# A three-stage convolution block on one core: one x tile per block of v, another order of loads, and products that nobody reads

## The chip, the cores and the metric

The kernel runs on one core of a Trainium2 chip. The metric is the time on the device in microseconds (us), the median of several runs. The core has four engines with instruction queues of their own: TensorE (PE: matrix products, and PEld: loads of their weights), VectorE (DVE), ScalarE (ACT) and GpSimd (POOL), and SyncE (SP), which here only starts DMA transfers. ACT and POOL start transfers too. [...]

## The reference: two residual blocks on one image

Input x has 384 channels of 192 x 192 float32. Group normalisation (32 groups of 12 channels) stands ahead of both blocks.

```python
def L0(x):                       # x = x + L0(gn(x))
    qkv = einsum('bchw,oc->bohw', x, w_qkv) + b_qkv        # 1x1, 384 -> 1152
    qkv = maxpool 2x2 (192 -> 96)
    qkv = depthwise 3x3 (qkv, w_dw) + b_dw
    q, k, v = split(qkv); q, k normalised over the pixels
    attn = q k^T * temperature   # 8 heads, 48 x 48 channels
    out = sum over 4 sizes of topk_softmax(attn, kk) @ v * a
    out = gelu(out); repeat each pixel 2 x 2
    return einsum('bchw,oc->bohw', out, w_proj) + b_proj
def L1(x):                       # x = x + L1(gn(x))
    w_sym = mean of the four rotations of weight
    return depthwise 7x7 (x, w_sym), padding 3
```

## The kernel before

Channels lie on the 128 partitions, in KT = 3 tiles. The program has stages, one after another on TensorE, with seams where they meet.

**Statistics and q, k.** x is read once for the mean and deviation of the first normalisation. Then, for 24 blocks of 8 image rows, TensorE forms q and k (`pq`, L639), VectorE takes the 2x2 maximum (L647) and the depthwise taps (`qk`, L682), ScalarE the squares for the norms (`junk`, L691), and TensorE transposes q and k (`tr`, L700) and adds their products to the attention's matrix (`grams`, L709). `depthwise(b - 1, ...)` runs a block behind. In the pass after the last block (b == NB) six groups of products of v are begun from a tile `xv_begun`, two after every second depthwise: `convolve(0, t0, n % KT, ...)`. A group is one call of `convolve`: 2 x 3 products of 384 columns (`pv`, L537) and one maximum (`rows`, L543).

**The attention**, a generator `attention`, is advanced by a few steps after each group of products of v: the norms' sum `rn` (L771), its root (POOL, L772), its reciprocal, `along_free` (L216), which lays three columns of rn along the free axis by three products with diagonal matrices (`dg_rk` L223, `af_rk` L224), the scaled matrix (L788), transfers that gather it by heads, ranks and softmaxes (`gt`, L813 and after), and its transpose `aT` (L857).

**v and the residual.** The image's 192 rows are cut in 6 tiles of 32 rows; a block is 2 rows of each of the 6 (NBC = 16 blocks). For each block three tiles `xv` of two row groups each are loaded (`load_v`, L876, three transfers of 384 KB each), and three tiles `xr` of one channel tile and all six row groups for the residual (`load_r`, L998, 1152 KB each). Both come from one pool of 6 places (tag "xv"), which the allocator hands out as they come free. Every x value of a block is thus read twice. Per iteration of the loop over i: convolutions of block i, depthwise taps `vb` (L903) of blocks i-1 and i-2, attention and projection of block j = i-2 (`po`, L959; `pr`, L983; `y`, L991), and its residual: `sx` = x + y (L1017, four additions for each channel tile, three `sx` buffers in turn), squares for the second statistics (ScalarE, L1037), and the writing of sx to DRAM (`sd`, L1058, and its halo rows `sh`), issued by POOL. After the loop come the last taps, all together, and the residuals of three blocks: NBC-2, NBC-1 and NBC (a wrap-around of the order).

**Second statistics.** Sums over groups by small products: `gs_mid` (L1237's input) and `gs`, both at L185; then `norm_of` (L211 to L215, with a power on POOL), and `along` (L1262), three times for channel tile 0: mean (`mb`), deviation (`sb`), its inverse (`rb`), each a diagonal on VectorE, a product `al` (L1266) and a copy. `masked` (L1271), `middle` (adds the deviation to the middle tap of w, L1253) and three rows of offsets (`offs`, L1294 and L1299, written by ScalarE's queue to h and to `wh`) follow.

**The 7x7 convolution**, 48 steps of 8 channels. A step has 4 groups q; a group forms 2 x 3 products of 288 columns into `pc`: w with main (L1389), w with main one column on (L1394), h with aux (L1400), in this order for each channel. `main` and `aux` come from sd and sh (`load_main`, `load_aux`), `w` and `h` from prepared weights; POOL corrects their borders (`borders`, L1310 to L1337), ScalarE copies rows of main into aux (`rest`, L1349) and columns of w into h (`columns`, L1187). Loads of steps 0 and 1 are issued by SP, later ones by ScalarE's queue (`queue`, L1161):

```python
        ws = {n: load_w(n) for n in range(2)}
        ws = {n: (ws[n], load_h(n)) for n in range(2)}
        auxes = {n: load_aux(n) for n in range(2)}
        mains = {n: (load_main(n), auxes[n]) for n in range(2)}
```

VectorE and ScalarE take the sums out of PSUM (`apart`, L1411, L1413), POOL interleaves them, SP writes them out.

**The order of work.** `keep` (or `pin`) makes an instruction stay in its place in the program; `tc.issue_after(x)` puts what is in it behind x; where neither stands, the order within an engine is chosen at build time by a planner from its own estimates of when operands are ready. A tile in a pool of n places waits for the release of the tile n earlier in its place.

## Time and profile before

| | us |
|---|---|
| median of 3 runs | 2817.28 (2816.37 to 2819.05) |
| profiled execution | 2823.79 |
| its span | 2822.1 |
| TensorE busy | 2640.9 (94%) |
| VectorE busy | 2320.9 (82%) |
| ScalarE, POOL busy | 870.5, 761.4 |

The profile shows one execution; its durations add up to the span of 2822.1, not to the median. PE and DVE are engines, "idle before" is the engine's idle time ahead of a group of instructions, and what follows the arrow is the instruction that ended it. PEclk is the TensorE clock granted, as a share of full speed: at half the clock a product takes twice as long. A line number is that of the kernel before. Products are recorded in two halves, so that x12 in a timeline of TensorE is six products of `convolve`.

The stages in the profiled execution: statistics up to about 120 us, q and k to about 1390, v and the residuals to 2217, the second statistics to 2230, the 7x7 steps to 2806, and the last results out until 2822.1.

### The profile page before, as it was taken

The page shows a single profiled execution, that of the slowest core. Times are in us where ns is not written, and L with a number is a line of the kernel's source. Part 1 is how long each engine was busy: PE and PEld are TensorE (multiplying, and loading weights), DVE is VectorE, ACT ScalarE, POOL GpSimd, SP SyncE. Part 2 cuts the span into 40 slices and gives each one's busy share as a digit, 9 for nine tenths or more (in the row PEclk, how much of TensorE's full clock was granted, in tenths as well). Part 3 has the DMA queues.
Part 4 walks back from the last instruction along what each step waited for, and adds up shares of the span by engine and source line. Part 5 has one row for each costly group of instructions (what it writes and reads, how often), then busy time and mean ns, then how long its engine had stood idle before and what let it go on. Part 6 is the DMA issues. An engine that isn't in the chain of part 4 may idle for free.

```text
span 2822.1 us, 25467 instructions
## 1 busy us (share of the span) xinstructions
PE 2640.9 (94%) x8671; PEld 1582.7 (56%) x8671; DVE 2320.9 (82%) x3382; ACT 870.5 (31%) x1637; POOL 761.4 (27%) x884
## 2 busy tenths in 40 slices
PE   0399999999999999999999999999998699999997
PEld 0144444444445444444556666666666477777775
DVE  7989887887878878778698888888889678777886
ACT  0141111111111111111202232322324567777775
POOL 1034444100000000000102230100101467888886
PEclk9999999999999999999999999999999799999999
DMA  9976766301001011010235998575666899999997
GB/s 377 400 244 219 258 200 219 126 34 67 34 34 67 34 51 50 34 67 1 80 124 189 332 376 293 199 251 179 235 207 224 301 304 362 372 373 370 373 373 248
DMA packets 236353, 584.52 MB, mean 207 GB/s; under 512 B 16656, under 2 KB 168064, under 8 KB 219456
## 3 DMA queue, kind: packets, MB, share of 16 engines
q1 hardware_dynamic: 175296, 286.77, 29.1%
q0 software_dynamic: 37376, 148.85, 15.2%
q10 hardware_dynamic: 23552, 147.27, 13.9%
q8 instruction: 69, 1.13, 0.2%
q14 instruction: 60, 0.49, 0.0%
HBM read 374.47 MB, written 208.21 MB: 206 GB/s over the span
## 4 chain that ended last, share of the span: by engine, by line
PE 89%; DVE 6%; DMA 3%; POOL 1%; issue 1%; ACT 0%; ACTq 0%; POOLq 0%; SPq 0%; DVEq 0%
PE pq L639 38%; PE pv L537 18%; PE pc L1400 6%; PE pc L1389 6%; PE pc L1394 6%; PE pr L983 4%; PE po L959 3%; DMA xs<-in_x_dram 2%; PE grams L709 2%; PE tr L700 2%; PE pq_begun L423 1%; DVE st L318 1%; DVE vb L903 1%; DVE sx L1017 1%; DMA bp<-in_bproj_dram 1%
## 5 line engine op out<-in xcount | busy, mean ns | idle before, releaser
L639 PE MATMUL pq<-xq,wq 128*128 128x512 f32 x2268 | 990.7, 592 | 0.0
L639 PEld LDWEIGHTS pq<-xq,wq 128*128 128x128 f32 x2268 | 423.2, 190 | 492.0 <-issue 446.8
L682 DVE SCALAR_TENSOR_TENSOR qk<-ring,wd,qk 128x384 f32<-128x384 f32 x1152 | 676.1, 615 | 20.9 <-ACT ring L669 7.1
L537 PE MATMUL pv<-xv,wq 128*128 128x384 f32 x1656 | 540.7, 487 | 3.2 <-DVE rows L543 3.0
L647 DVE TENSOR_REDUCE ring<-pq 128x128 f32<-128x512 f32 x428 | 294.7, 689 | 190.5 <-PE pq L639 188.8
L537 PEld LDWEIGHTS pv<-xv,wq 128*128 128x128 f32 x1656 | 314.8, 190 | 218.3 <-DVE rows L543 5.0
L1413 DVE TENSOR_SCALAR apart<-pc,rb 32x576 f32<-32x576 f32 x384 | 312.0, 813 | 125.7 <-PE pc L1400 111.4
L1411 ACT ACTIVATE apart<-pc,rb 32x576 f32<-32x576 f32 x384 | 281.1, 732 | 144.5 <-PE pc L1400 139.7
L903 DVE SCALAR_TENSOR_TENSOR vb<-rows,wd,vb 128x576 f32<-128x576 f32 x384 | 313.3, 818 | 11.3
L1400 PE MATMUL pc<-aux,h 128*128 128x288 f32 x768 | 250.9, 408 | 2.7 <-POOL aux L1322 2.7
L1389 PE MATMUL pc<-main,w 128*128 128x288 f32 x768 | 251.4, 409 | 0.3 <-issue 0.3
L1394 PE MATMUL pc<-main,w 128*128 128x288 f32 x768 | 251.3, 409 | 0.0
L1017 DVE TENSOR_TENSOR sx<-xr,y 128x576 f32<-128x576 f32 x192 | 217.4, 1173 | 33.8 <-ACT y L991 21.4
L691 ACT ACTIVATE junk<-qk 128x384 f32<-128x384 f32 x144 | 75.3, 523 | 548.8 <-DVE qk L682 548.8
L801 POOL MEMSET lower<- 128x2304 f32 x1 | 2.0, 2017 | 881.1 <-ACT rows L508 881.1
L1359 POOL COPY res<-apart 128x1152 f32<-128x1152 f32 x96 | 210.0, 2222 | 87.2 <-DMA out_dram<-res 61.0
L1058 POOL DMA_DIRECT2D sd<-sx x96 | 72.2, 756 | 491.8 <-DVE sx L1017 474.2
L543 DVE TENSOR_REDUCE rows<-pv 128x192 f32<-128x768 f32 x144 | 137.8, 957 | 54.2 <-PE pv L537 54.1
L1400 PEld LDWEIGHTS pc<-aux,h 128*128 128x128 f32 x768 | 146.3, 191 | 45.5 <-POOL aux L1322 3.5
L1394 PEld LDWEIGHTS pc<-main,w 128*128 128x128 f32 x768 | 146.7, 191 | 41.9
L1389 PEld LDWEIGHTS pc<-main,w 128*128 128x128 f32 x768 | 146.4, 191 | 41.9 <-issue 0.6
L1037 ACT ACTIVATE wq<-sx,negmid 128x1152 f32<-128x1152 f32 x96 | 120.6, 1256 | 96.6 <-DVE sx L1017 92.5
(216 smaller groups left out, 2384.5 us busy)
## 6 DMA issues: line engine op xcount, KB each, us to landing
sd<-sx POOLq DMA_DIRECT2D x96, 600.0 KB, 10.1
xr<-in_x_dram SPq DMA_DIRECT2D x48, 1152.0 KB, 14.1
out_dram<-res SPq DMA_DIRECT2D x192, 288.0 KB, 8.4
main<-sd ACTq DMA_DIRECT2D x46, 1200.0 KB, 9.8
xv<-in_x_dram SPq DMA_DIRECT2D x138, 384.0 KB, 5.4
xq<-in_x_dram SPq DMA_DIRECT2D x21, 2304.0 KB, 8.2
w<-wt ACTq DMA_DIRECT2D x46, 1024.0 KB, 6.6
xs<-in_x_dram SPq DMA_DIRECT2D x24, 1536.0 KB, 15.1
```

Of the source, the lines that this page charges most:

```text
L537: nc.tensor.matmul(ps[:, u, 0 : RB * HW], wq[:, kt, o : o + P], xb[:, kt, u, :], start=(kt == 0), stop=(kt == KT - 1),)
L639: nc.tensor.matmul(ps, wq[:, kt, ct * P : (ct + 1) * P], rows[:, kt, :, g * 64 : (g + 1) * 64], start=(kt == 0), stop=(kt == KT - 1), skip ...
L647: nc.vector.tensor_reduce(t[:, r0 : r0 + PR, 1 + g * 32 : 1 + (g + 1) * 32], ps.rearrange("p (h a w b) -> p h w a b", h=PR, a=2, b=2), AX. ...
L682: nc.vector.scalar_tensor_tensor(dst, src, w, dst, ALU.mult, ALU.add)
L903: pin(nc.vector.scalar_tensor_tensor(dst, src, w, dst, ALU.mult, ALU.add))
L1017: nc.vector.tensor_tensor(bass.AP(flat.tensor, flat.offset + at(e) + a * RUN, [flat.ap[0], [JP, NT], [1, NJ], [at(f) - at(e), 2]],), xq[:, ...
L1359: keep(nc.gpsimd.tensor_copy(res[:, k], apart[:, :, k].rearrange("p e n -> p n e")))
L1389: nc.tensor.matmul(acc, w[:, i, 0:P], main[:, i, :, 0:NJ], start=True, stop=False)
L1394: nc.tensor.matmul(acc, w[:, i, P : 2 * P], main[:, i, :, 1 : 1 + NJ], start=False, stop=False,)
L1400: nc.tensor.matmul(acc, h[:, i], aux[:, i, :, 0:NJ], start=False, stop=True,)
L1411: keep(nc.scalar.mul(dst, src, scale))
L1413: keep(nc.vector.tensor_scalar_mul(dst, src, scale))
```

## The change

- **The seam from q, k to v.** The six begun groups are called at ct = 2 (two), ct = 4 (two), ct = 5 and ct = 6 (one each), inside `issue_after(multiplied)`: `multiplied` is the last gram of block 22 up to ct = 5, and that of block 23 at ct = 6, so five groups come behind the one and the sixth behind the other. `rn` moves to the pool of constants, and the diagonal `dg` has three buffers instead of two.
- **x of v.** One tile `xv` with a fixed place for each pair of row groups takes the place of the xv tiles out of the common pool; `xr` has a pool of 3. The residual of the last block in the loop's order reads its x from this tile, and its three xr loads are gone. In `xv_begun` and `xv` the row groups are the outer index and the channel tiles the inner one.
- **The last taps.** The taps dy = 0 of block NBC come after the second residual of block NBC-2.
- **The first loads of the 7x7 stage.** SP now issues w0, h0, h1, aux0, main0, w1, aux1, main1; before it was w0, w1, h0, h1, aux0, aux1, main0, main1. The three transfers of offsets go from ScalarE's queue to SP's.
- **Products nobody reads.** `busy` forms products of the resident projection weights into a PSUM tile of its own: 16 after gs_mid, 2 before the al of the mean, 2 before that of the deviation, 3 before that of its inverse.
- **Step 0.** Groups 0 and 1 form all their products of w and main (eight) before those of h and aux.

Places and counts that follow from these in the build, per engine: VectorE has as many instructions as before, TensorE 23 products more; POOL clears two of the three h tiles ahead of its last six sd transfers; VectorE forms the deviation's diagonal and the first offsets ahead of the copy of mb, and the other offsets and rb ahead of the middle taps of w.

The diff, with one line of context:

```diff
@@ -219,7 +219,7 @@
         for t in range(KT):
-            dg = const.tile([P, P], F32, name=f"dg_{name}_{t}", tag="dg", bufs=2)
+            dg = const.tile([P, P], F32, name=f"dg_{name}_{t}", tag="dg", bufs=KT)
             nc.vector.tensor_scalar_mul(dg, ident, src[:, t : t + 1])
@@ -535,7 +535,7 @@
                     nc.tensor.matmul(
-                        ps[:, u, 0 : RB * HW], wq[:, kt, o : o + P], xb[:, kt, u, :],
+                        ps[:, u, 0 : RB * HW], wq[:, kt, o : o + P], xb[:, u, kt, :],
                         start=(kt == 0), stop=(kt == KT - 1),
@@ -729,9 +729,9 @@
                 pv = psx.enter_context(tc.tile_pool(name="pv", bufs=2, space=PSUM))
-                xb = xpool.tile([P, KT, 2 * UT, RB * HW], F32, name="xv_begun", tag="xb")
+                xb = xpool.tile([P, 2 * UT, KT, RB * HW], F32, name="xv_begun", tag="xb")
                 for kt in range(KT):
-                    nc.sync.dma_start(xb[:, kt], image_rows(kt, order[0], 0, 2 * UT))
+                    nc.sync.dma_start(xb[:, :, kt], image_rows(kt, order[0], 0, 2 * UT))
             qk = []
@@ -748,12 +748,13 @@
                     depthwise(b - 1, ct - 1, dst)
-                    if b == NB and ct % 2 == 0:
-                        for n in range(ct - 2, ct):
-                            t0 = n // KT * UT
-                            convolve(0, t0, n % KT, xb[:, :, t0 : t0 + UT], lambda ins: ins)
                     if ct == 2 * KT:
                         multiplied = products(b - 1, qk)
+                    if b == NB:
+                        with tc.issue_after(multiplied):
+                            for n in ((), (), (0, 1), (), (2, 3), (4,), (5,))[ct]:
+                                t0 = n // KT * UT
+                                convolve(0, t0, n % KT, xb[:, t0 : t0 + UT], lambda ins: ins)
             if b == 2:
@@ -767,7 +768,7 @@
-        rn = ap.tile([P, 2 * KT], F32, name="rn")
+        rn = const.tile([P, 2 * KT], F32, name="rn")
         nc.vector.tensor_reduce(rn, ssq, AX.X, ALU.add)
@@ -866,7 +867,9 @@
     vp = dx.enter_context(tc.tile_pool(name="vp", bufs=6))
-    xp2 = dx.enter_context(tc.tile_pool(name="xp2", bufs=6))
+    xp2 = dx.enter_context(tc.tile_pool(name="xp2", bufs=3))
+    xvp = dx.enter_context(tc.tile_pool(name="xvp", bufs=1))
+    xvs = xvp.tile([P, NT, KT, RB * HW], F32, name="xv")
     H = PBC // 2
@@ -874,10 +877,9 @@
     def load_v(i, t0):
-        b = order[i]
-        xb = xp2.tile([P, KT, UT, RB * HW], F32, name=f"xv{b}_{t0}", tag="xv")
+        xb = xvs[:, t0 : t0 + UT]
         for kt in range(KT):
-            nc.sync.dma_start(xb[:, kt], image_rows(kt, b, t0, UT))
+            nc.sync.dma_start(xb[:, :, kt], image_rows(kt, order[i], t0, UT))
         return xb
@@ -996,7 +998,10 @@
     def load_r(i, ot):
-        xr = xp2.tile([P, NT, RB * HW], F32, name=f"xr{order[i % NBC]}_{ot}", tag="xv")
+        if i == NBC - 1:
+            return xvs[:, :, ot]
+        xr = xp2.tile([P, NT, RB * HW], F32, name=f"xr{order[i % NBC]}_{ot}", tag="xr")
         nc.sync.dma_start(xr, image_rows(ot, order[i % NBC], 0, NT))
@@ -1105,7 +1110,8 @@
-    for j, dys in ((NBC - 2, (2,)), (NBC - 1, (0, 1)), (NBC, (0,))):
+    for j, dys in ((NBC - 2, (2,)), (NBC - 1, (0, 1))):
         for ct in range(KT):
@@ -1119,6 +1125,9 @@
             next(after[ot])
+            if (j, ot) == (NBC - 2, 1):
+                for ct in range(KT):
+                    depthwise_v(NBC, ct, (0,), keep)
         before = after
@@ -1160,9 +1169,8 @@
-            if n < 2:
-                return nc.sync.dma_start
-            return lambda dst, src: keep(nc.scalar.dma_start(dst, src))
+            engine = nc.sync if n < 2 else nc.scalar
+            return lambda dst, src: keep(engine.dma_start(dst, src))
@@ -1197,10 +1205,13 @@
-        ws = {n: load_w(n) for n in range(2)}
-        ws = {n: (ws[n], load_h(n)) for n in range(2)}
-        auxes = {n: load_aux(n) for n in range(2)}
-        mains = {n: (load_main(n), auxes[n]) for n in range(2)}
+        ws, mains = {0: load_w(0)}, {}
+        hs = [load_h(n) for n in range(2)]
+        for n in range(2):
+            ws[n] = ws[n] if n == 0 else load_w(n), hs[n]
+            aux = load_aux(n)
+            mains[n] = load_main(n), aux
@@ -1231,10 +1242,17 @@
         rstd1 = const.tile([P, KT], F32, name="rstd1")
+        def busy(ps, n):
+            for _ in range(n):
+                keep(nc.tensor.matmul(ps[:, 0:H], wp[:, 0, 0:P], wp[:, 1, 0:H], start=True, stop=True))
         with tc.tile_pool(name="gps1", bufs=1, space=PSUM) as gps:
             nc.vector.tensor_scalar_mul(gmid, ps[:, :, 0], 1.0 / GC)
+            busy(gps.tile([P, 512], F32, name="busy"), 16)
             ps = over_groups(gps, about(mv1, gmid, "1"), 2, "gs1")
@@ -1277,10 +1295,14 @@
+        idle = pc.tile([P, 2, 512], F32, name="idle", tag="pc")
+        busy(idle[:, 0], 2)
         along(mb, mean1, 0)()
+        busy(idle[:, 0], 2)
         masked(0)
         along(sb, std1, 0)()
+        busy(idle[:, 0], 3)
         middle(0)
@@ -1293,11 +1315,11 @@
         for n in ws:
-            nc.scalar.dma_start(ws[n][1][ONE : ONE + 1], offs[span(n), 0, :])
+            nc.sync.dma_start(ws[n][1][ONE : ONE + 1], offs[span(n), 0, :])
         along(rb, rstd1, 0)()
             nc.vector.tensor_scalar_mul(offs[:, kt, :], ones, off1[:, kt : kt + 1])
-        nc.scalar.dma_start(wh[ONE - TOP].rearrange("(t p) n -> p t n", p=P), offs)
+        nc.sync.dma_start(wh[ONE - TOP].rearrange("(t p) n -> p t n", p=P), offs)
@@ -1380,28 +1402,32 @@
             apart = outp.tile([P, CP, 2, NT * NJ], F32, name=f"apart{n}", tag="apart", bufs=3)
-            for q in range(CP):
-                ps = pc.tile([P, 2, 512], F32, name=f"pc{n}_{q}", tag="pc")
+            ahead = {}
+            def sums(q, steps):
+                if q not in ahead:
+                    ahead[q] = pc.tile([P, 2, 512], F32, name=f"pc{n}_{q}", tag="pc")
                 for k in range(2):
                     i = 2 * q + k
-                    acc = ps[:, k, 0 : NT * NJ]
-                    keep(
-                        nc.tensor.matmul(
-                            acc, w[:, i, 0:P], main[:, i, :, 0:NJ], start=True, stop=False
+                    for j in steps:
+                        lhs, rhs = (
+                            (w[:, i, j * P : (j + 1) * P], main[:, i, :, j : j + NJ]) if j < 2
+                            else (h[:, i], aux[:, i, :, 0:NJ])
                         )
-                    )
-                    keep(
-                        nc.tensor.matmul(
-                            acc, w[:, i, P : 2 * P], main[:, i, :, 1 : 1 + NJ],
-                            start=False, stop=False,
+                        keep(
+                            nc.tensor.matmul(
+                                ahead[q][:, k, 0 : NT * NJ], lhs, rhs,
+                                start=(j == 0), stop=(j == 2), skip_group_check=True,
+                            )
                         )
-                    )
-                    keep(
-                        nc.tensor.matmul(
-                            acc, h[:, i], aux[:, i, :, 0:NJ],
-                            start=False, stop=True,
-                        )
-                    )
+                return ahead[q]
+            if n == 0:
+                for q in range(2):
+                    sums(q, range(2))
+            for q in range(CP):
+                ps = sums(q, range(2 if q in ahead else 0, 3))
                 c = n * CB + 2 * q
                     src = ps[g * TR : (g + 1) * TR, :, 0 : NT * NJ]
```

## The prediction

> **What bounds the kernel now.** I read the page's busy shares and slices first, to find out which engine sets the time and where it doesn't, then its groups.
>
> ```profile
> PE 2640.9 (94%) x8671; PEld 1582.7 (56%) x8671; DVE 2320.9 (82%) x3382; ACT 870.5 (31%) x1637; POOL 761.4 (27%) x884
> PE   0399999999999999999999999999998699999997
> PEclk9999999999999999999999999999999799999999
> L537 PE MATMUL pv<-xv,wq 128*128 128x384 f32 x1656 | 540.7, 487 | 3.2 <-DVE rows L543 3.0
> L1017 DVE TENSOR_TENSOR sx<-xr,y 128x576 f32<-128x576 f32 x192 | 217.4, 1173 | 33.8 <-ACT y L991 21.4
> ```
>
> TensorE is full nearly everywhere: from 1500 to 2140 us its busy time is 640.00 of 640.00, from 2294 to 2806 it is 512.00 of 512.00. An edit there pays only if it shortens TensorE's own work. Time can be won at the seams: the change from q,k to v (1390 to 1450), and slices 30 and 31 (2117 to 2258, the 8 and the lone 7 of PEclk), with the end of v, the second statistics and the first 7x7 step.
>
> Seam one, TensorE's timeline (start, length, line, count, idle before and its releaser):
>
> ```profile
> 1368.99 19.51 PE L537 MATMUL pv<-xv_begun,wq 128*128 128x384 f32 x60
> 1388.34 1.67 PE L700 MATMUL tr<-ident,qk 128*128 128x128 f32 x12
> ...
> 1401.28 1.19 PE L224 MATMUL af_rk<-dg_rk,ones 128*128 128x128 f32 x4 [3.89 <-DVE dg_rk L223]
> ...
> 1403.97 39.79 PE L537 MATMUL pv<-xv,wq 128*128 128x384 f32 x120
> 1446.80 3.49 PE L537 MATMUL pv<-xv,wq 128*128 128x384 f32 x10 [3.05 <-DVE rows L543]
> ```
>
> Two stalls, 3.89 and 3.05. What holds dg_rk is seen on ScalarE and VectorE:
>
> ```profile
> 1388.54 0.51 ACT L508 ACTIVATE rows<-ones,negb 128x16 f32<-128x16 f32 x2 [7.49 <-PE pv L537]
> ```
>
> ```profile
> 1394.35 0.30 DVE L771 TENSOR_REDUCE rn<-ssq 128x6 f32<-128x144 f32 x1 [4.85 <-ACT rows L508]
> ```
>
> The norms' sum rn waits for border fills, though its last square was done at 1381.05; the attention's first big operation (gt, L813) starts only at 1410.13.
>
> Seam two, VectorE's residual additions sx:
>
> ```profile
> 2169.06 13.53 DVE L1017 TENSOR_TENSOR sx<-xr,y 128x576 f32<-128x576 f32 x12
> 2184.48 4.61 DVE L1017 TENSOR_TENSOR sx<-xr,y 128x576 f32<-128x576 f32 x4 [1.89 <-DMA sd<-sx]
> ...
> 2200.65 4.58 DVE L1017 TENSOR_TENSOR sx<-xr,y 128x576 f32<-128x576 f32 x4 [2.20 <-DMA sd<-sx]
> 2206.73 4.55 DVE L1017 TENSOR_TENSOR sx<-xr,y 128x576 f32<-128x576 f32 x4 [1.50 <-ACT wq L1037]
> 2212.44 1.15 DVE L1017 TENSOR_TENSOR sx<-xr,y 128x576 f32<-128x576 f32 x1 [1.17 <-DMA sd<-sx]
> ```
>
> The last ends at 2217.0. Three sx buffers go round, and each waits until its write to sd has landed; the DMA share is 1.01 (2200 to 2216). Behind it hangs everything, on TensorE's timeline:
>
> ```profile
> 2201.93 2.00 PE L185 MATMUL gs_mid<-mid,gsel 128*128 128x1 f32 x14 [2.33 <-ACT y L991]
> 2219.23 3.15 PE L185 MATMUL gs<-about,gsel 128*128 128x2 f32 x14 [15.30 <-DVE about L205]
> ...
> 2234.74 1.30 PE L1400 MATMUL pc<-aux,h 128*128 128x288 f32 x2 [2.70 <-POOL aux L1322]
> ...
> 2240.63 0.72 PE L1400 MATMUL pc<-aux,h 128*128 128x288 f32 x2
> ```
>
> After 15.30 us idle the granted clock is 0.50 from 2205 to 2240: a 7x7 product takes 0.96 us until 2240.8, then 0.485. From 2293.64 on nothing waits, so a microsecond won before that is won at the end.
>
> **The change, part by part.**
>
> *One xv tile, three xr buffers.* Products, loads and bytes per block stay; only the row order inside the tile turns, and a product still reads 384 elements in a row (487 ns). Each place is reloaded once per block (50.35 us) and waits only for the last product that read the same place a block before; from the order on SP's queue each load has 38 us or more of lead against a landing of 5.4: 0. The last block's residual reads x from the tile: three loads of 1152 KB fall away, 3 x 1152 KB at 376 GB/s = 9.4 us of DMA time near 2102 to 2165, hidden there, but lightening the stretch whose landings hold sx.
>
> *The seam q,k to v.* Of six begun groups (3.87 us each) five now come before the last block's transposes and the sixth after its grams; rn no longer waits for the fills and the depthwise has two instead of three reduces of 0.96 between its taps. rn can be summed at 1381.1; with POOL's power (1.36) and two small operations it is there at 1384, long before TensorE asks. Five groups end as before at about 1388.3; transposes, tps and grams take 5.3 (5.7, less one transpose trio done earlier), af_rk 1.0, groups six and 13_4_0 7.74: 13_4_1 starts at 1402 instead of 1403.97, **-2.0**. The fourth group's place is taken by waiting (the first group no longer fills gaps between block 22's transposes, 3.9 us), which is why the 3.89 isn't won whole. The attention chain starts some 10 us earlier (rkb and scaled right after af_rk, then the same 4 us of att DMAs), on a VectorE that idles 17 us between 1381 and 1410; the stall at 1446.80 comes from that chain's lateness and goes: **-3.0**. Together -5.0; bounds -2 (the stall stays) and -6.5.
>
> *The end of v.* Nine taps of block NBC (7.4 us; vb L903 at 0.82) move behind two residuals. VectorE's work is the same: 33 taps from 2142.0 (27.2) and 36 additions of 1.155 (41.6) end at 2210.8 if nothing waits; now it is 2217.0. sx starts at 2161.6; buffers come round by 4.5 us of additions, with the nine taps in the second turn, so the fourth and fifth residuals find landings of 10 us done; from the sixth on 1 to 4 us of waiting remain at 9.6 to 12.8 us a landing. I take 2.5: the end is 2213.3, **-3.7** (-1 to -6).
>
> *Loads of the first steps.* SP's order is now w0, h0, h1, aux0, main0, then w1, aux1, main1. main0 waits for the sd writes, and 2.8 MB now stand behind that wait: 7.5 us at 376 GB/s. With main0 issued by 2213 to 2216 they land by 2227; POOL asks for main1 at 2231.53 and VectorE for w1 at 2242.28, so 0; 5 us later they would bind. The three offset DMAs go from ScalarE's queue to SP, whose next work is the outputs: ScalarE's copies for step 0 (they stood 13.02 us idle behind offs L1299) start 0.9 us earlier. POOL clears h0 and h1 before the last sd issues, in idle of 5 us, so that the power no longer stands behind six memsets: -0.4.
>
> *Products nobody reads.* 16 after gs_mid, then 2, 2 and 3 ahead of the three al products. Shape 128x288 as pc: 0.485 warm, 0.96 cold. 16 take 7.8 to 15.4 us from about 2200; gs can't start before 2215.5, so they fit unless all are cold. What they buy hangs on the clock. The row: after 2234.74 the clock came back in 6.1 us of unbroken products. [...] By the row the 16 take 6.1 + 9.6 x 0.485 = 10.8[...]: done by 2211, so TensorE idles 4 us before gs[...]: the clock may have fallen again. The trace agrees (the 3.57 us idle at 2144.66 is followed by 0.52). I take gs as cold (3.15, no gain) and the seven small ones, with al, as dense work from the norms to step 0, 7 us, which by the row wakes it: step 0 warm. Cold they delay rb by 1 us: **+0.5**. If the clock holds, gs is 1.1 shorter.
>
> *Step 0.* Eight products of w and main come first; aux is wanted 3.9 us (warm) after the first, and comes 4.1 after: the 2.70 becomes 0.2. VectorE now makes three small operations and the first offsets ahead of mb (about 1 us), rb ahead of w: w comes within 0.8 us of before, taken as 0. Steps 0 to 2 take 42.1 us from 2229.78, at 0.485 they are 34.9: 7.2 lost, 2.7 by the wait and 4.5 by the clock. **-6.0** warm (7.2 less 0.2 and a last half-cold stretch of 1), -3.5 cold.
>
> Sum: -5.0 - 3.7 - 0.4 + 0.5 - 6.0 = -14.6. The profiled execution takes 2823.79 (span 2822.1 and 1.7 around it), 6.5 above the median of the runs, 2817.28; so 2809.2 in its terms and **2802.7 us** as a median.
>
> **Rivals.** *Half of it*: the landings still pace sx (DMA share 1.01 speaks for it) and step 0 is cold: -5 - 1 - 3.5 + 1 = -8.5, 2808.8. *Nothing*: 1446's stall stays, the dummies run cold to 2215.4 and hold gs, w1 and main1 arrive late by 3 to 5 us: -2 - 1 + 2 - 3.5 + 4 = -0.5, 2816.8. *More*: landings free sx wholly and the cold stretch at 2276 (2.9 us, after step 2's al) goes as well: -20, 2797. *Slower*: SP's queue is in order, and a v load stands behind xr loads that wait for a residual a block back. If a load landed later than its 38 us of lead, each of 13 iterations would stall. From (14.6 + 5.6)/13 = 1.6 us apiece the kernel is slower; at the 5.4 us of a whole load it is +70 - 15, 2872. Against it: VectorE, which releases xr, idles 74 of 640 us in the loop.
>
> **How the numbers follow.** Forecast 0.60 (own range 2798 to 2807), half 0.20, more 0.06, nothing 0.08, slower 0.06. The measurement can tell 0.2%, 5.6 us: faster below 2811.6, slower above 2822.9. Forecast, more, and most of half are faster: 0.85; same 0.09, slower 0.06. The range, 2795 to 2812, leaves out nothing and slower and a little of more.
>
> **What would show it.** rn near 1381; no stall over 1 us near 1440, aT near 1480 (before 1485.61). sx ends 2 to 5 us nearer the last tap of v. No 15 us idle before gs, but one of 2 to 5; the first pc at 0.485, no aux wait over 1. From step 3 the same 11.64 a step. It is wrong if TensorE in the v loop is no longer full, if pc starts at 0.96, or if the wait moves to w1 or main1.

## The result and the profile after

The changed kernel takes 2804.3 us (median of 5 runs, 2802.2 to 2807.42) against 2818.65 for the kernel before beside it: ratio 0.9948, 95% interval 0.9936 to 0.996, or 14.35 us. The forecast was 14.6 us and 2802.7. The profiled execution has a span of 2802.6; that of before had 2822.1, 19.5 more. The 5 us beyond the medians' difference come from the choice of execution: the profiled one of before (2823.79) lies 5.1 above this median, that of the changed kernel (2804.3) is its median.

The page of the changed kernel, its busy shares and slices:

```profile
PE 2647.1 (94%) x8717; PEld 1586.9 (57%) x8717; DVE 2352.2 (84%) x3382; ACT 870.7 (31%) x1637; POOL 745.6 (27%) x884
...
PE   0399999999999999999999999999999899999997
...
PEclk9999999999999999999999999999999999999999
```

TensorE is busy 6.2 us longer, for 23 products more and others warmer or colder, and the 7 of PEclk is gone. TensorE's timeline at the seam from q, k to v (start, length, line, count, idle before it and what ended it):

```profile
1364.45 19.51 PE L537 MATMUL pv<-xv_begun,wq 128*128 128x384 f32 x60
1383.80 1.04 PE L700 MATMUL tr<-ident,qk 128*128 128x128 f32 x8
...
1388.49 0.94 PE L224 MATMUL af_rk<-dg_rk,ones 128*128 128x128 f32 x6
...
1403.21 47.02 PE L537 MATMUL pv<-xv,wq 128*128 128x384 f32 x144 [1.36 <-DVE rows L543]
```

The 3.89 at af_rk is gone, and so is the 3.05 at 1446.80; a new wait for rows, of 1.36, stands at 1403.21. VectorE there:

```profile
1377.13 0.29 DVE L772 TENSOR_REDUCE rn<-ssq 128x6 f32<-128x144 f32 x1
...
1395.03 4.79 DVE L814 TENSOR_TENSOR gt<-att 128x2304 f32<-128x2304 f32 x1
```

rn no longer waits for the fills, and gt starts at 1395.03 instead of 1410.13; since the last q,k product is 5.4 us earlier in this execution, 9.7 of the 15.1 are the seam's. (gt takes 4.79 here and 2.56 before; POOL works on `lower`, L803, beside it, from 1394.93 to 1397.40.) VectorE's residual additions after the loop:

```profile
2162.18 7.39 DVE L905 SCALAR_TENSOR_TENSOR vb<-rows,wd,vb 128x576 f32<-128x576 f32 x9
...
2186.76 4.62 DVE L1022 TENSOR_TENSOR sx<-xv,y 128x576 f32<-128x576 f32 x4 [3.81 <-DMA sd<-sx]
2192.70 10.06 DVE L1022 TENSOR_TENSOR sx<-xr,y 128x576 f32<-128x576 f32 x9 [1.33 <-DMA sd<-sx]
```

The nine taps stand between the residuals, and two waits for landings remain, 5.1 us. The second statistics and step 0 on TensorE:

```profile
2195.41 9.69 PE L1249 MATMUL busy<-wp 128*128 128x288 f32 x32
2208.36 2.53 PE L185 MATMUL gs<-about,gsel 128*128 128x2 f32 x14 [3.26 <-DVE about L205]
2211.15 2.29 PE L1249 MATMUL idle<-wp 128*128 128x288 f32 x4 [0.26 <-DVE norm L211]
...
2215.96 1.62 PE L1249 MATMUL idle<-wp 128*128 128x288 f32 x6
...
2219.26 4.12 PE L1419 MATMUL pc<-main,w 128*128 128x288 f32 x16 [1.46 <-POOL aux L1352]
2223.38 2.18 PE L1419 MATMUL pc<-aux,h 128*128 128x288 f32 x8
```

The 15.30 us of idle are 3.26, the 16 products (32 halves) take 9.69, the eight of step 0 take 4.12, 0.51 apiece, and those of aux follow without a wait.

Laid side by side by stages, with a second trace of each kernel (the runs e1 and e5 below), in us:

| stage | before | before again | changed | changed again |
|---|---|---|---|---|
| start to first q,k product | 122.5 | 121.5 | 121.5 | 122.0 |
| to the end of the last one (first tr of block 22) | 1237.8 | 1238.1 | 1233.3 | 1231.4 |
| to aT | 125.4 | 125.0 | 122.3 | 120.7 |
| to the first tap after the loop | 656.4 | 656.4 | 656.4 | 662.6 |
| to the end of the last sx | 75.0 | 75.1 | 72.6 | 72.7 |
| to the first pc | 12.8 | 12.8 | 13.1 | 12.2 |
| to the end of step 2 | 42.1 | 42.1 | 35.4 | 35.4 |
| to the end | 550.2 | 551.0 | 547.9 | 548.7 |

### The profile page after: what moved, and what is told of

The parts are those of the page before. It is cut to its first block, busy times and chain, and to the rows that moved or that the text cites. A ratio compares the mean times of both kernels' runs of the same rounds, so it can differ in the third digit from the quotient of the medians.

```text
span 2802.6 us, 25628 instructions
## 1 busy us (share of the span) xinstructions
PE 2647.1 (94%) x8717; PEld 1586.9 (57%) x8717; DVE 2352.2 (84%) x3382; ACT 870.7 (31%) x1637; POOL 745.6 (27%) x884
## 3 DMA queue, kind: packets, MB, share of 16 engines
q8 instruction: 69, 1.13, 0.2%
## 4 chain that ended last, share of the span: by engine, by line
PE 89%; DVE 6%; DMA 3%; issue 1%; POOL 0%; ACT 0%; ACTq 0%; POOLq 0%; SPq 0%; DVEq 0%
PE pq L639 37%; PE pv L537 20%; PE pc L1419 20%; PE pr L985 4%; PE po L961 3%; DMA xs<-in_x_dram 2%; PE grams L709 2%; PE tr L700 2%; PE pq_begun L423 1%; DVE qk L682 1%; DVE st L318 1%; DVE sx L1022 1%; DVE vb L905 1%; DMA bp<-in_bproj_dram 1%; DMA sd<-sx 0%
## 5 line engine op out<-in xcount | busy, mean ns | idle before, releaser
L1419 PE MATMUL pc<-main,w 128*128 128x288 f32 x1536 | 434.8, 405 | 1.8 <-POOL aux L1352 1.5
L905 DVE SCALAR_TENSOR_TENSOR vb<-rows,wd,vb 128x576 f32<-128x576 f32 x384 | 313.2, 817 | 11.2
L1381 POOL COPY res<-apart 128x1152 f32<-128x1152 f32 x96 | 222.6, 2344 | 21.6 <-ACT apart L1437 18.9
L1022 DVE TENSOR_TENSOR sx<-xr,y 128x576 f32<-128x576 f32 x180 | 203.6, 1173 | 27.3 <-ACT y L993 21.3
L1271 DVE SCALAR_TENSOR_TENSOR w<-eye,sb,w 128x512 f32<-128x512 f32 x96 | 168.0, 1789 | 1.5
L1419 PEld LDWEIGHTS pc<-aux,h 128*128 128x128 f32 x768 | 144.9, 189 | 42.1 <-issue 0.9
L985 PE MATMUL pr<-gl,wp 128*128 128x288 f32 x576 | 142.6, 406 | 0.0
```

Source lines behind the costliest of these rows:

```text
L905: pin(nc.vector.scalar_tensor_tensor(dst, src, w, dst, ALU.mult, ALU.add))
L985: nc.tensor.matmul(ps[:, 0:H], wp[:, ct, ot * P : (ot + 1) * P], gl[:, ct, h * H : (h + 1) * H], start=(ct == 0), stop=(ct == KT - 1),)
L1022: nc.vector.tensor_tensor(bass.AP(flat.tensor, flat.offset + at(e) + a * RUN, [flat.ap[0], [JP, NT], [1, NJ], [at(f) - at(e), 2]],), xq[:, ...
L1271: nc.vector.scalar_tensor_tensor(mid, eye.unsqueeze(1).to_broadcast([P, 4, P]), sb[:, c : c + 1], mid, ALU.mult, ALU.add,)
L1381: keep(nc.gpsimd.tensor_copy(res[:, k], apart[:, :, k].rearrange("p e n -> p n e")))
L1419: nc.tensor.matmul(ahead[q][:, k, 0 : NT * NJ], lhs, rhs, start=(j == 0), stop=(j == 2), skip_group_check=True,)
```

## The experiments

The ratios are to the kernel before, timed beside each. Its median was 2818.65, 2818.82, 2831.78, 2828.02 and 2817.81 us in the five groups of runs, so that times of different groups aren't compared; the stages of the traces are the finer gauge.

| run | ratio (95%) |
|---|---|
| changed | 0.9948 (0.9936 to 0.996) |
| e1 before again | 0.9997 (0.9987 to 1.0008) |
| e2 no products | 0.9964 (0.9952 to 0.9976) |
| e3 groups back | 0.9939 (0.9923 to 0.9954) |
| e4 taps back | 0.9973 (0.9963 to 0.9984) |
| e5 changed again | 0.9932 (0.9909 to 0.9955) |
| e6 rn back | 0.9981 (0.9968 to 0.9994) |
| e7 loads back | 0.9932 (0.9906 to 0.9958) |
| e8 step 0 back | 0.9953 (0.9941 to 0.9965) |
| e9 xv back | 0.9966 (0.9953 to 0.9978) |
| e10 xr by POOL | 0.9955 (0.9942 to 0.9967) |
| e11 groups back, xr by POOL | 0.9942 (0.9928 to 0.9955) |
| e12 no sixteen | 0.9956 (0.994 to 0.9972) |

### Both kernels a second time (e1, e5)

> The kernel before, unchanged, for a second trace. The two profiled executions differ by 19.5 us in span, the medians by 14.35; 4.4 us of the difference lie between the first q,k product and the last one, which no part of the change touches (two stalls there in the trace of before, 2.08 at L639 and 1.74 at L700). Theory A, they are the chance of one execution: here the time from the first pq_begun to the last pq is 1233 to 1236 us in place of 1237.8, and the span near 2817. Theory B, the new build's order or addresses removed them: the two stalls come back and the span is again near 2822.

> The changed kernel, unchanged, beside the next three, and for a second trace. By the six traces so far the time from the first pq_begun to the last pq is of two kinds in kernels whose code up to there is the same (1231 to 1233 us in two, 1237 to 1238 in four). Theory A, it is the chance of an execution: the median is again 2804 (2802 to 2806), whichever kind the trace shows. Stages after it, as in the first trace: last pq to first tap vb after the loop 778 to 780, from there to the last sx 72.6, sx to the first pc 13, steps 0 to 2 35.4. Theory B, a build's addresses decide it: the trace shows 1233 again.

Before again has 1238.1 us from first to last q,k product and both stalls (2.08 and 1.96), so e1's theory A, as put, fell. Its theory B forecast them, but that the new build had removed them by its order fell with e2, e4, e8, e11 and e12: in their traces, with the code of the changed kernel up to there, this stage takes 1237 to 1238 too, and in seven others with that code 1231 to 1234.

What the stalls are can be read from the traces. VectorE and POOL of before at the second one, then VectorE of changed again at the same instruction:

```profile
338.24 2.20 DVE L680 TENSOR_SCALAR qk<-ring,wd,bdb 128x384 f32<-128x384 f32 x1
```

```profile
338.05 2.18 POOL L566 MEMSET g<- 128x2496 f32 x1 [8.71 <-DMA wt<-g]
```

```profile
333.00 0.48 DVE L680 TENSOR_SCALAR qk<-ring,wd,bdb 128x384 f32<-128x384 f32 x1
```

By itself this operation takes 0.46 to 0.48 us in all fourteen traces. In before it starts at 338.24, inside POOL's memset (338.05 to 340.23, which prepares weights of the 7x7 stage), and ends at 340.44, 0.21 us behind it, and TensorE waits for what follows. In the first traces of the two kernels all twelve operations of this line that start inside such a memset end behind it. The first stall stands in eleven of the fourteen traces, and the operation takes 1.87 to 2.55 us there; the second in seven, with 2.20 to 2.48; where a stall is missing, it takes 0.82 at most in the same place. Who goes first is a matter of nanoseconds: at the first stall the operation starts 0.148 us ahead of the memset in before and takes 2.54; in the changed kernel it starts 0.160 ahead and takes 0.48, and the memset takes 2.43 instead of 2.18. Throughout the fourteen traces a start up to 0.157 ahead was held, and one from 0.160 on was not.

With neither stall the stage takes 1231.4 to 1233.3 (the changed kernel twice, e3), with the first alone 1233.7 to 1233.9 (e6, e7, e9, e10), with both 1237.2 to 1238.1. Up to 1300 us the instructions of all four engines stand in the same order in all fourteen traces, so no edit acts there; what differs is when two operations meet. Each of the two kernels showed its own kind twice, so whether the executions of one kernel change between the kinds isn't shown. That stays open, and with it some 5 us of the difference between the traces.

Changed again has a median of 2813.48, outside e5's 2802 to 2806, but before took 2831.78 beside it; the ratio is 0.9932, where it was 0.9948. And it brought what I had set at 0: the loop takes 662.6 instead of 656.4. TensorE's timeline of e5:

```profile
1666.68 0.88 PE L537 MATMUL pv<-xv,wq 128*128 128x384 f32 x2 [1.88 <-DMA xv<-in_x_dram]
1668.50 25.74 PE L537 MATMUL pv<-xv,wq 128*128 128x384 f32 x70 [0.93 <-DMA xv<-in_x_dram]
```

SP's queue in the same execution:

```profile
1613.94 22.39 SPq L1005 DMA_DIRECT2D xr<-in_x_dram  x3
1636.42 34.10 SPq L882 DMA_DIRECT2D xv<-in_x_dram  x9
```

The first of these xv loads, from the view of its line between 1636 and 1637:

```profile
DMA to landing us min/median/max: 30.1/30.1/30.1
```

The place was free when the product group before it ended, at 1626 (1614.29 and a group of 11.6). The load stood behind three xr loads waiting for sx until 1636.4, and landed at 1666.5, when TensorE had been waiting since 1664.8. So the lead of 38.8 us was there, as predicted; 10.4 of it went to SP's queue and 30.1 to a landing put at 5.4. After the 1.88 us of idle the clock was down, as the sums over three stretches show (length; busy time of PE, PEld, DVE, ACT, POOL with counts; the granted clock; DMA share and GB/s):

```profile
1664.13:1667.54 3.41, 1.53 (x5) 0.49 (x3) 3.36 (x4) 2.79 (x5) 2.96 (x4) 1.00 1.06 404
1667.54:1674.37 6.83, 5.90 (x10) 3.12 (x10) 1.16 (x1) 2.22 (x6) 3.75 (x6) 0.50 1.06 399
1674.37:1684.00 9.63, 9.63 (x31) 5.72 (x30) 7.73 (x8) 2.70 (x4) 1.67 (x3) 1.00 1.02 376
```

Half of 6.83 us and the 2.8 of idle are the 6.2 us that the loop lost. Among seven traces with this loop's code (the changed kernel twice, e2, e4, e7, e8, e12) the stage takes 656.4, 662.6, 659.0, 657.5, 659.1, 666.1 and 656.4: 3.2 over before on the mean, and where TensorE waits, it is always at this one iteration (1666 to 1680).

### The seam: groups and rn (e3, e6)

e3:

```diff
+                    if b == NB and ct % 2 == 0:
+                        for n in range(ct - 2, ct):
+                            t0 = n // KT * UT
+                            convolve(0, t0, n % KT, xb[:, t0 : t0 + UT], lambda ins: ins)
                     if ct == 2 * KT:
                         multiplied = products(b - 1, qk)
-                    if b == NB:
-                        with tc.issue_after(multiplied):
-                            for n in ((), (), (0, 1), (), (2, 3), (4,), (5,))[ct]:
-                                t0 = n // KT * UT
-                                convolve(0, t0, n % KT, xb[:, t0 : t0 + UT], lambda ins: ins)
```

e6:

```diff
-            dg = const.tile([P, P], F32, name=f"dg_{name}_{t}", tag="dg", bufs=KT)
+            dg = const.tile([P, P], F32, name=f"dg_{name}_{t}", tag="dg", bufs=2)
...
-        rn = const.tile([P, 2 * KT], F32, name="rn")
+        rn = ap.tile([P, 2 * KT], F32, name="rn")
```

> The changed kernel with the six begun groups of v placed as before (two after every second depthwise, free among block 22's transposes), rn and dg as in the changed kernel. Theory A, by the two traces: the first group fills 3.5 us of gaps among the transposes of block 22, and with rn early nothing waits for dg_rk any more, so the 3.89 us idle doesn't come back: 2 to 3.5 us faster than the changed kernel, near 2801.5. Theory B, the group order is what starts the attention early: the stalls at dg_rk and at rows return, 2 to 3 us slower, near 2807.

> The changed kernel with rn again in the attention's own pool and two places for dg; the groups' places as in the change. Theory A, rn's early sum is what the seam won: rn waits for the fills again, the attention starts some 8 us later, and TensorE stalls at dg_rk or at rows by 3 us more: last pq to first tap 782, 2807. Theory B, the groups' order won it: no difference, 779, 2804.

From the last q,k product to aT:

| | rn late | rn early |
|---|---|---|
| groups as before | 125.4, 125.0 (before) | 118.3 (e3), 118.4 (e11) |
| groups as changed | 129.0 (e6) | 120.7 (seven traces), 122.3 |

The changed kernel's own first trace is the 122.3: its clock stood at 0.50 for 3.41 us behind the last q,k product (1359.16 to 1362.57), which is the 1.7 more. e9 (125.7) is left out here, since a load is late in it.

rn and dg together are worth 8.4 us with the new groups (e6), and 6.8 with the old ones, where the comparison of e3 with before holds the rest of the change too; the new places of the groups cost 2.4. Theory A holds in both, and in e6 the effect is larger than the 3 us I expected. VectorE, then TensorE, of e6:

```profile
1389.38 0.30 DVE L772 TENSOR_REDUCE rn<-ssq 128x6 f32<-128x144 f32 x1 [4.81 <-PE grams L709]
```

```profile
1396.30 1.19 PE L224 MATMUL af_rk<-dg_rk,ones 128*128 128x128 f32 x4 [3.24 <-DVE dg_rk L223]
```

Counted from the last q,k product, rn is formed 12.6 us later than in changed again (1374.07), and the stall stands before the first product of af_rk, which the late rn holds and not the number of places of dg. The two were not put back one by one, though.

e3 has a median of 2801.94, against 2804.3 for the changed kernel in another group of runs; the intervals of the ratios overlap, so by time it isn't shown to be faster, by the stage it is.

### The last taps (e4)

```diff
-    for j, dys in ((NBC - 2, (2,)), (NBC - 1, (0, 1))):
+    for j, dys in ((NBC - 2, (2,)), (NBC - 1, (0, 1)), (NBC, (0,))):
...
-            if (j, ot) == (NBC - 2, 1):
-                for ct in range(KT):
-                    depthwise_v(NBC, ct, (0,), keep)
```

> The changed kernel with the nine taps of block NBC ahead of the residuals, as before. Theory A: sx starts 7.4 us later, the waits for landings stay as long, and the last sx ends 2 to 2.5 us later against the last convolution of v: 2806.5. Theory B, the landings pace the residuals whatever stands ahead of them, or the three xr loads taken away made room: no difference, 2804.

First tap to last sx: 74.5 us, against 72.6 with the taps moved and 75.0 before. So of the 2.4 won 1.9 are the taps', and theory A holds. That the other 0.5 is the lighter traffic isn't shown: with the three xr loads back (e9) the stage takes 72.7, and the traces with the taps moved lie between 71.3 and 72.9. The time is 7 us above that of the changed kernel by the ratios, more than the stage shows; in this trace the eight products of step 0 also ran half cold (5.81 instead of 4.12) and the q,k stage is of the longer kind (1237.2), but whether the timed executions were like it isn't known.

### The products nobody reads (e2, e12)

e2 leaves out all of these, e12 the first alone:

```diff
-            busy(gps.tile([P, 512], F32, name="busy"), 16)
...
-        idle = pc.tile([P, 2, 512], F32, name="idle", tag="pc")
-        busy(idle[:, 0], 2)
         along(mb, mean1, 0)()
-        busy(idle[:, 0], 2)
         masked(0)
         nc.vector.reciprocal(std1, rstd1)
         along(sb, std1, 0)()
-        busy(idle[:, 0], 3)
```

> The changed kernel without the 23 products that nobody reads. Theory A, they are worth the clock at step 0: the first pc products take 0.96 for 5 to 8 us, steps 0 to 2 take 38 to 39 us from the first pc (35.4 with them), the clock dips at the al of the second channel tile once more (2.9), less 1.0 as the three al come sooner: 3 to 5 us slower than the changed kernel, near 2808. Theory B, the eight w and main products first do it alone: no slower, 2803 to 2805.

> The changed kernel without the 16 products after gs_mid; the seven ahead of the al stay. Theory A, as the prediction has it: the idle before gs lets the clock fall whether or not the 16 ran, and the seven with al, about 7 us of dense work, wake it again: gs 3.15 (1.7 to 2.5 with the 16), the first eight products of step 0 in 4 to 5.8 us (4.1 to 5.8 with the 16, 6.8 without all 23), steps 0 to 2 35.4 to 36.8, the time as the changed kernel's or 1 us more. Theory B, the 16 shorten the cold stretch of the seven: without them the seven are cold to the end, the first pc comes 1 to 2 us later against the last sx (12.9 with the 16), and the eight take 6 to 7.7: 3 to 4 us slower.

Step 0 on TensorE, e2 first:

```profile
2224.29 6.76 PE L1414 MATMUL pc<-main,w 128*128 128x288 f32 x16 [2.31 <-POOL aux L1339]
```

```profile
2211.14 3.15 PE L185 MATMUL gs<-about,gsel 128*128 128x2 f32 x14 [12.11 <-DVE about L205]
...
2222.23 4.12 PE L1418 MATMUL pc<-main,w 128*128 128x288 f32 x16 [1.07 <-POOL aux L1343]
```

Without the 23, steps 0 to 2 take 38.5 us instead of 35.4, as e2's theory A has it. Without the 16 alone, 35.3: the seven wake the clock by themselves (granted 0.50 from 2200 to 2215, 0.58 to 2220, then 1.00). gs is then 3.15 instead of 1.7 to 2.5, but the first pc comes 13.3 after the last sx against 12.2 to 13.1. Theory A of e12 holds to the numbers; the ratios of e12 and the changed kernel overlap, so a gain from the 16 is not shown. That the cold stretch at the al comes back without the products (e2's theory A) isn't shown: it comes and goes from one execution to the next, 18.9 us from the end of step 2 to that of step 3 in one trace of before and 14.2 in the other.

### Step 0's order (e8)

```diff
-            if n == 0:
-                for q in range(2):
-                    sums(q, range(2))
```

> The changed kernel with step 0's products channel by channel, as before. Theory A: the third product wants aux 1 us after the first, and aux comes 4.1 us after: 2.7 to 3.2 us of waiting, steps 0 to 2 38 to 38.6, 2807. Theory B, moving the offsets to SP has already made aux early: no wait, 35.4, 2804.

TensorE of e8:

```profile
2235.89 1.22 PE L1419 MATMUL pc<-aux,h 128*128 128x288 f32 x2 [2.84 <-ACT aux L1371]
```

2.84 us of waiting (by ScalarE's part of aux), and behind it the products are slow:

```profile
2236.91 2.12 PE L1419 MATMUL pc<-main,w 128*128 128x288 f32 x4
...
2239.59 1.13 PE L1419 MATMUL pc<-main,w 128*128 128x288 f32 x4
```

These four halves take 2.12 us, and the same four 1.13 from 2239.59 on. Steps 0 to 2 take 39.9 instead of 35.4: theory A, with 1.3 to 1.9 more than it allows.

### The first loads (e7)

```diff
...
-        ws, mains = {0: load_w(0)}, {}
-        hs = [load_h(n) for n in range(2)]
...
+        ws = {n: load_w(n) for n in range(2)}
+        ws = {n: (ws[n], load_h(n)) for n in range(2)}
+        auxes = {n: load_aux(n) for n in range(2)}
+        mains = {n: (load_main(n), auxes[n]) for n in range(2)}
...
-            nc.sync.dma_start(ws[n][1][ONE : ONE + 1], offs[span(n), 0, :])
+            nc.scalar.dma_start(ws[n][1][ONE : ONE + 1], offs[span(n), 0, :])
...
-        nc.sync.dma_start(wh[ONE - TOP].rearrange("(t p) n -> p t n", p=P), offs)
+        nc.scalar.dma_start(wh[ONE - TOP].rearrange("(t p) n -> p t n", p=P), offs)
```

e7 also lets the planner place these loads again (`queue`, not shown here): it puts three things back at once.

> The changed kernel with the loads of steps 0 and 1 in the old order and the offsets on ScalarE's queue. Theory A, worth little: w1 and aux1 (1.6 MB, 4.3 us at 376 GB/s) lie again in the stretch whose landings hold sx, so the last sx is 0.5 to 1 later, and ScalarE's copies for step 0 0.9 later, which the eight products cover for the most part: 1 to 2 us slower, 2805.5. Theory B, the order of loads is what freed sx: sx's end 2.4 later (75 us from the first tap), 2807 and more.

Neither theory: from the first tap after the loop to the end of step 2 e7 takes 118.8 us, the changed kernel 121.1 and 120.3. sx ends 71.3 after the first tap, not later (why, no run shows), and the first pc follows 9.7 after it instead of 12.2 to 13.1; then aux is 2.45 late. By time the two don't differ (both 0.9932 in the same group of runs).

In all fourteen traces the first pc starts 0.1 us after VectorE ends its first operation on w, so w sets it. VectorE of e7, of the changed kernel, and of e12:

```profile
2215.38 3.41 DVE L1270 SCALAR_TENSOR_TENSOR w<-eye,sb,w 128x512 f32<-128x512 f32 x2
2218.71 0.28 DVE L1284 COPY rb<-al 128x128 f32<-128x128 f32 x1
```

```profile
2216.37 1.93 DVE L1321 TENSOR_SCALAR offs<-ones,off 128x128 f32<-128x128 f32 x2
2218.22 0.28 DVE L1285 COPY rb<-al 128x128 f32<-128x128 f32 x1
2218.42 1.64 DVE L1271 SCALAR_TENSOR_TENSOR w<-eye,sb,w 128x512 f32<-128x512 f32 x2
```

```profile
2219.84 3.12 DVE L1270 SCALAR_TENSOR_TENSOR w<-eye,sb,w 128x512 f32<-128x512 f32 x2
2222.89 0.28 DVE L1284 COPY rb<-al 128x128 f32<-128x128 f32 x1
```

In e7 w comes 0.5 us after the copy of sb; in the changed kernel the last offsets and rb, which waits for its own al, stand ahead of it, and w comes 2.3 us after sb (2.7 in changed again). Counted from the last sx, w is 2.5 to 3.5 us earlier in e7; about 2 of them are this order, the rest the clock, which stayed at 1.00 from 2205 to 2235, with TensorE busy for 9.74 of the first 10 us. The offsets' queue doesn't fix the order: e12 has the offsets on SP and w ahead of rb all the same. It gains nothing by it, since its sb comes 10.6 us after the last sx, with the clock at 0.50 from 2200 to 2215 and at 0.58 to 2220, and its first w takes 2.3 us instead of 0.7. The changed kernel with w put ahead of rb and nothing else was not run.

### The xv tile, and who issues xr (e9, e10, e11)

e9:

```diff
-    xp2 = dx.enter_context(tc.tile_pool(name="xp2", bufs=3))
-    xvp = dx.enter_context(tc.tile_pool(name="xvp", bufs=1))
-    xvs = xvp.tile([P, NT, KT, RB * HW], F32, name="xv")
+    xp2 = dx.enter_context(tc.tile_pool(name="xp2", bufs=6))
...
-        xb = xvs[:, t0 : t0 + UT]
+        xb = xp2.tile([P, UT, KT, RB * HW], F32, name=f"xv{order[i]}_{t0}", tag="xv")
...
-        if i == NBC - 1:
-            return xvs[:, :, ot]
...
-        xr = xp2.tile([P, NT, RB * HW], F32, name=f"xr{order[i % NBC]}_{ot}", tag="xr")
+        xr = xp2.tile([P, NT, RB * HW], F32, name=f"xr{order[i % NBC]}_{ot}", tag="xv")
```

e10, and e11 together with the edit of e3:

```diff
-        nc.sync.dma_start(xr, image_rows(ot, order[i % NBC], 0, NT))
+        nc.gpsimd.dma_start(xr, image_rows(ot, order[i % NBC], 0, NT))
```

> The changed kernel with xv and xr again in one pool of six places and with the last block's three xr loads. In five of the eight traces of kernels with the single xv tile TensorE waits 0.3 to 6.0 us for xv near 1670, in both traces of before it doesn't. Theory A, the single tile leaves no load ahead: there the wait is gone, from aT to the last product of v 655.5 to 656.5 us (655.5 to 665 with the tile), and the last sx comes 0.5 to 1.5 later against the first tap (72.6 with the tile): 1 to 3 us faster than the changed kernel on the same chip. Theory B, the wait is that of any kernel with an early attention in this stretch of full DMA queues: it stays.

> The changed kernel with the xr loads issued by POOL, behind the sd writes of the block before, in place of SP. Theory A, the loads of xv come late because they stand behind xr loads on SP's queue that wait for sx (22 to 24 us near 1615 to 1640): no wait for xv near 1670, aT to the last product 655.5 to 656.5. Theory B, the transfers themselves are slow there (18 to 29 us from issue to landing, the DMA share above 1.0 from 1580 to 1700): the wait stays at 2 to 6 us in some executions. If POOL's own transfers land later than SP's, the residuals are late and the tail is longer than 72.6.

> Both at once: the begun groups free among block 22's transposes, and xr issued by POOL. Theory A: the 3.3 us of the groups and the wait for xv add up: last pq to first tap 775 to 776 in every execution, 5 us under the changed kernel, near 0.9925 of before. Theory B, an earlier attention shifts the loads into the full stretch: the gain is that of the groups alone or less.

With the pool of six the wait isn't gone. TensorE of e9:

```profile
1687.52 0.91 PE L537 MATMUL pv<-xv,wq 128*128 128x384 f32 x2 [3.38 <-DMA xv<-in_x_dram]
1691.91 12.77 PE L537 MATMUL pv<-xv,wq 128*128 128x384 f32 x32 [3.48 <-DMA xv<-in_x_dram]
```

From aT to the first tap it takes 666.0 us, and a further 3.74 is lost at the seam, where a load for the first products after the six begun groups now comes late (aT 125.7 after the last q,k product). The last sx comes 72.7 after the first tap, not later as theory A had it. Theory A fell: the wait is there without the single tile, as theory B forecast. (Of the eight traces that the expectation counts, six show the wait.) With xr on POOL's queue the wait for xv is gone and another has its place; VectorE and TensorE of e10:

```profile
1673.01 9.01 DVE L1022 TENSOR_TENSOR sx<-xr,y 128x576 f32<-128x576 f32 x8 [11.66 <-DMA xr<-in_x_dram]
```

```profile
1682.85 17.13 PE L537 MATMUL pv<-xv,wq 128*128 128x384 f32 x48 [7.21 <-DVE rows L543]
```

VectorE waits 11.66 us for xr, the maximum behind it comes late, and the loop takes 666.3 (e11: 667.7). e11 so gave back what the groups had won, as its theory B says. The reading that fits these runs is that the transfers' time is short in this iteration (DMA share 1.04 from 1580 to 1700 in the first trace of each kernel), and that whichever load has the least lead pays; no run made room there to test it. In the two traces of before nothing waits there. Which of the change's shifts uses up that slack isn't settled: e6, with the attention late, waits too (663.6), so theory B's reason, an early attention, isn't it either; the turned order of rows in xv, which e9 keeps, was never put back.

## Why the prediction was right, by its own steps

| step | forecast | traces |
|---|---|---|
| seam q,k to v | -5.0 | -4.5 (120.7 against 125.2) |
| one xv tile, in the loop | 0 | +3.2 on the mean (0 to 9.7) |
| the end of v | -3.7 | -2.4 |
| products nobody reads, and POOL | +0.1 | 0 (12.2 and 13.1 against 12.8) |
| step 0 | -6.0 | -6.7 |
| after step 2 | 0 | -2.3 (two traces of each) |
| sum | -14.6 | -12.7 |

The median moved by 14.35; the q,k stage's kinds, which lie up to 6.7 us apart, can cover the rest, and no run tells how much of it the medians hold. That the sum came within 0.3 us of the median is in part luck: misses of +3.2 and +1.3 stand against -2.3 after step 2, which nothing forecast (two traces of each kernel lie between 547.9 and 551.0, and steps 3 and 4 alone vary from 30.2 to 33.6), and against what the q,k stage gave.

**The seam** went as reckoned, with rn's early sum as its cause and the groups' places as a cost (e3, e6). The price named for them, the 3.9 us no longer filled, is 2.4 net.

**One xv tile: the term that was mis-sized.** "Each load has 38 us or more of lead against a landing of 5.4: 0" took the landing from a median over the whole run. Where the load matters it is 30.1, and 10.4 us stand behind xr on SP. The rival named *slower* described this mechanism, with the right queue; it happens in one iteration of 13, not in all, so that it costs 3 us and not that rival's 70. e9 says, moreover, that it isn't the tile's alone; what the change used up there stays open.

**The end of v** won less: two waits of 5.1 us were left where I had taken 2.5. That is 2.6 less; 1.3 of it came back, since taps and additions themselves took 67.5 us (72.6 less 5.1) instead of the 68.8 reckoned.

**The clock.** That 6.1 us of unbroken products bring the clock back was my estimate, from one row of before; the record of the granted clock has it back at 2240.77, 6.03 us after 2234.74. The runs don't show one length for it: in the changed kernel the 16 begin at 2195.41 and the clock is at 0.50 from 2195.42 to 2198.83, 3.41 us. The times at which it changes, 15 in the trace of before and 13 in that of the changed kernel, lie whole multiples of 3.41 us apart. The 16 took 9.69 us; the estimate by the row was 10.8. Over the ten traces that have the 16 it is 9.5 to 9.7 in seven and 10.5 to 11.1 in three (e4, e7, e9), where the clock stood at 0.50 for 6.83 us there instead of 3.41.

For the fall the runs show no one length of idle either: in e5 the clock fell after 3.41 us with TensorE busy for 1.53 of them. And before, it fell at 2203.22, ahead of the 15.30 us of idle that the prediction names as the cause (they begin at 2203.93), behind 2.33 of idle and within the small products of gs_mid.

The forecast said that the 16 would be undone by the idle before gs and that the seven would wake the clock again. So it was: the changed kernel's clock is at 0.50 from 2209.07, within gs, to 2215.90, and then at 1.00; it falls again in nine of the ten traces with the 16, and e12 shows it by leaving them out. In e5 and e3 the idle before gs was only 2.1 and 2.0 us and gs stayed warm (1.72), but the clock fell behind it.

**Step 0** is as reckoned: of the gain of 6.7, 3.1 go with the products (e2) and 4.5 with the order (e8). The two overlap: behind the 2.84 us of waiting in e8 four halves take 2.12 us instead of 1.13.

**The first loads** were set at 0, and w came "within 0.8 us of before" as forecast: 12.2 and 11.2 us after the last sx, against 11.9. But VectorE's order behind it hid a loss: with w ahead of rb it comes about 2 us sooner (e7).

## What to carry to other kernels

Take the landing of a transfer from the stretch in which its load is issued (30.1 us here, in e5), and add the wait of what stands before it on its queue (10.4); the median over the run before, with light and full stretches, was 5.4 and said nothing of the lead that was needed. Of the dummy products here, the few that stand last before the work paid; the 16 with an idle between them and the work were not shown to. A chain's late start is worth hunting for what it waits for by mere place in memory: moving one small tile to another pool, with one more place for another, brought 8.4 us here, and reordering the large groups cost 2.4. And where a stage differs that the change doesn't touch, see whether two operations of VectorE and POOL meet there in one trace and not in the other (2.20 us for one of them in before, 0.48 in changed again).

## What the runs showed of the hardware

- Loads of 384 KB that land in 5.4 us at the median of the run before (6.3 in the changed kernel) took 13 to 35 us when issued between 1580 and 1690 (the first trace of each), where the DMA share is 1.04.
- The granted clock changed 15 times in the trace of before and 13 times in that of the changed kernel, at times whole multiples of 3.41 us apart. In e5 it stood at 0.50 for 6.83 us (1667.54 to 1674.37) after a stretch of 3.41 us with 1.53 us of products, and the loop lost 6.2 us, with 2.8 of idle.
- A tensor_scalar of 128x384 on VectorE takes 0.46 to 0.48 us by itself (fourteen traces) and 1.87 to 2.55 at the places where TensorE waits for it, beside a memset of 128x2496 on POOL of 2.18. An operation that started up to 0.157 us ahead of the memset was held by it, one that started 0.160 or more ahead was not.
